# A hybrid attention layer on one core: another attention loop and another spectral loop

## The chip, the cores and the metric

The kernel runs on one core of a Trainium2 chip. The metric is the device time of one execution in microseconds, the median of several runs. In the text PE is TensorE (matmuls), PEld its weight loads, DVE is VectorE, ACT is ScalarE, POOL is GpSimd, and SP is the engine that issues most of the DMAs. SBUF is the on-chip memory of 128 partitions; PSUM holds eight banks of 512 float32 for each partition, into which matmuls write. All data are float32.

## What is computed

The input is four images of 56x56 pixels with 128 channels. One layer adds neighbourhood attention to it, the next adds linear attention and then a convolution with sixteen long filters. Cut to its core:

```python
# x: (4, 56, 56, 128)
q, k, v = heads(gn(x) @ qkv_w.T + qkv_b)              # 4 heads of 32
a = softmax(q . k[7x7 window] * 32**-0.5 + bias)      # 49 weights per pixel
x = x + (a . v[7x7 window]) @ proj_w.T + proj_b

t = tokens(x)                                         # (4, 3136, 128)
n = layernorm(t)
q, k, v = exp(n @ Wq + bq), exp(n @ Wk + bk), n @ Wv + bv
t = t + q @ (k.T @ v)

u = layernorm(t)
for i, frac in enumerate((1, 2, 4, 8)):               # experts, one is chosen
    xi = u[:, : T // frac]
    U_plus, U_minus = fft_convolutions(phi, xi)       # 16 filters each
    s_i = (U_plus * sigma**0.25) @ M_plus[i] + (U_minus * sigma**0.25) @ M_minus[i]
    s_i = s_i + sum(shift(xi, j) @ M_u[i, j] for j in range(3))
t = t + sum_i weight_i * pad(s_i)                     # weights: one-hot
```

## The kernel before

The work has three parts.

**The main part**, image by image (the loop of L928): `project` normalises an image by its groups and makes the queries `qT`, the padded keys `kp` in SBUF and the values, which go to memory as `vpad`. `attend` walks over 35 tiles: 7 rows of tiles with four of 8x12 pixels and one of 8x8. A tile of 96 queries meets 14x18 = 252 keys, in two halves of 126. `mix` adds the projected attention (`add_tokens`, L548 to 557), normalises (`normed`), makes `kv` and `q2` (linear attention), adds that, normalises again, and adds the three taps under the mask `tmask`. `row_transforms` of an image is the first step of its convolution: 7 groups of matmuls L509, each pair of results `xs` going to memory as `xd`. It is a generator; the kv loop of the next image's `mix` takes a step of it every second turn (L896), and the last image's steps run alone.

PSUM in this part is three pools of two buffers: `ps_s` has two pairs of banks, `ps_t` and `ps_m` two single banks each. `bank()` gives project and mix their banks in a turn of three: two from `ps_s`, whose pairs it splits, and one from `ps_m`.

In `attend` a tile goes through these steps: `score` (L738, four matmuls, one per head, into two pairs `sp`); `soften` (L755 adds the bias and takes the negated maximum on DVE; L766 is the exp on ACT, with the sum of a row); `turn_over` (L797, eight transposes into two banks `pt`); `keep_weights` (L808: DVE copies the first half to SBUF, ACT the second); `invert` (L780 reciprocal, L782 a copy on POOL that spreads it, `wide`); `collect` (L819, sixteen matmuls with the values `v_sb`, and L826, which turns `wide` over to the channels), after which DVE copies `rb` (L834) and multiplies into `aT` (L835). The order of PE, DVE, ACT and POOL is written out by hand here (L844): in turn n a tile n+2 is loaded, n-2 is turned over, n is softened in two halves with `keep_weights(n - 2)` between them, n-1 inverted, n-3 collected, and n+1 scored. Everywhere else a scheduler chooses the order of an engine's instructions.

`normed` collects the means and variances of four blocks, then makes their factors at once on DVE with two operations on POOL (L585 and L586, a power), then those of the other three, and normalises all blocks on ACT (L597).

**The spectral loop** (L1070) has 42 iterations, one for each frequency row, and three more to run out. Iteration `it` makes the matrices of the filters, `gt`, for `it`: in each of eight turns `eh`, `matrices` issues 16 matmuls (32 instructions in the profile) into two pairs of banks `pg`, one pair copied by DVE and one by ACT (L1006). `token_points` (L979) transforms the tokens into `us`. `product` (L1016) multiplies `gt` and `us` of iteration `it - 1`: two matmuls for each of 56 points, four instructions in the profile, with 16 columns of `us` as the weights and 128 of `gt` as the moving operand; `j = m2 % 4` chooses the 32 rows of the result. `gather` (L1029) copies 16 rows at a time to `ys`, which goes through memory (`regroup`) to `yg`, and `columns` (L1052) of iteration `it - 3` transforms back to `zs`, which is stored. PE's order is written out by hand.

**The last part** (L1107 on) transforms the rows back and adds the result.

Of the kernel before, what the change touches and what calls it, by code (L numbers as in the profile page):

```python
# [120 lines left out]
def hybrid_kernel(  # L121
# [252 lines left out]
    with main as ph:  # L374
# [5 lines left out]
        ps_s = ph.enter_context(tc.tile_pool(name="ps_s", bufs=2, space=bass.MemoryType.PSUM, reuse_waits="tile"))  # L380
        ps_t = ph.enter_context(tc.tile_pool(name="ps_t", bufs=2, space=bass.MemoryType.PSUM, reuse_waits="tile"))
        ps_m = ph.enter_context(tc.tile_pool(name="ps_m", bufs=2, space=bass.MemoryType.PSUM, reuse_waits="tile"))

        turn, pair = [0], []

        def bank():

            turn[0] = (turn[0] + 1) % 3
            if turn[0] == 2:
                return ps_m.tile([P, 512], F32, tag="m", name="bm")  # L390
            if not pair:
                two = ps_s.tile([P, 2, 512], F32, tag="s", name="bs")
                pair.extend((two[:, 1, :], two[:, 0, :]))
            return pair.pop()
# [98 lines left out]
        def row_transforms(b):  # L493
# [10 lines left out]
            yield  # L504
            for i in range(BR // 4):
# [10 lines left out]
                for s in range(NS):  # L516
                    xs = work.tile([2 * N1, 2, 4, C], F32, name="xs", bufs=2)
                    evacuate(xs.rearrange("p h w c -> p h (w c)"), px[s][: 2 * N1])
                    for wh in range(2):
                        w0 = wh * BR + 4 * i  # L520
                        nc.sync.dma_start(xd[:, w0 : w0 + 4, s, b, :], xs[:, wh])
                yield
# [46 lines left out]
        def normed(acc, add, to):  # L569


            stats = small.tile([P, 2 * NB, 6], F32, name="stats", bufs=2)
            nc.gpsimd.memset(stats[:, 2 * NB - 2 :], 1.0)

            def factors(g0, g1):

                s, n = stats[:, g0:g1], g1 - g0
                v = small.tile([P, 4, 16], F32, name="v")
                total, d, rstd, shift = (v[:, i, :n] for i in range(4))

                nc.vector.tensor_tensor(d, s[:, :, 1], s[:, :, 4], ALU.subtract)
                nc.vector.tensor_tensor(rstd, s[:, :, 2], s[:, :, 5], ALU.add)
                nc.vector.scalar_tensor_tensor(d, d, C / 4.0, d, ALU.mult, ALU.mult)
                nc.vector.tensor_tensor(rstd, rstd, d, ALU.add)
                nc.gpsimd.tensor_scalar(rstd, rstd, 1.0 / C, LN_EPS, ALU.mult, ALU.add)  # L585
                nc.gpsimd.tensor_tensor(rstd, rstd, mhalf[:, :n], ALU.pow)  # L586
                nc.vector.tensor_tensor(total, s[:, :, 1], s[:, :, 4], ALU.add)
                nc.vector.scalar_tensor_tensor(shift, total, -0.5, rstd, ALU.mult, ALU.mult)  # L588
                return rstd, shift

            def normalize(js, g0, rstd, shift):
                r = rows_of(js[0])
                hn = work.tile([P, 2, 2, C], F32, name="hn", bufs=3)
                for g in range(2 * len(js)):
                    jj, f = divmod(g, 2)
                    at = 2 * js[0] - g0 + g
# [4 lines left out]
                        bias=shift[:r, at : at + 1],  # L601
                        scale=rstd[:r, at : at + 1],
# [3 lines left out]
            parts = []  # L606
            for run in (BLOCKS[:4], BLOCKS[4:]):
                for js in run:
                    add(js)
                    r = rows_of(js[0])  # L610
                    for j in js:
                        for f in range(2):
                            nc.vector.bn_stats(
                                stats[:r, 2 * j + f, :], acc[:r, j, f * C : (f + 1) * C]
                            )
                g0, g1 = 2 * run[0][0], 2 * run[-1][-1] + 2
                parts.append((run, g0, *factors(g0, g1)))
            for run, *args in parts:
                for js in run:
                    normalize(js, *args)  # L620
# [91 lines left out]
        def attend(b, qT):  # L712
# [7 lines left out]
            def load(n):  # L720

                ty, x0, qc = tiles[n]
                kc, y0 = qc + KS - 1, ty * QR
                v_sb = work.tile([KMAX, 2, C], F32, name="v_sb", bufs=6)
                for c in range(2):
                    nc.sync.dma_start(
                        v_sb[: KH * kc, c], vpad[b, y0 + c * KH : y0 + (c + 1) * KH, x0 : x0 + kc]
                    )
                state[n] = {"v": v_sb, "nq": QR * qc, "kn": KH * kc}

            def score(n):
                ty, x0, qc = tiles[n]
                t = state[n]
                nq, kn, y0 = t["nq"], t["kn"], ty * QR
                t["sp"] = [ps_s.tile([P, 2, 512], F32, tag="s", name="sp") for _ in range(2)]
                for h in range(NH):
                    hs = slice(h * HD, (h + 1) * HD)
                    nc.tensor.matmul(  # L738
                        t["sp"][h // 2][:nq, h % 2, : 2 * kn],
                        qT[hs, ty, QR * x0 : QR * x0 + nq],  # L740
                        kp[hs, y0 : y0 + KR, x0 : x0 + qc + KS - 1],
# [3 lines left out]
                t["st"] = work.tile([NQ, NH, NK], F32, name="st", bufs=3)  # L745
                t["nmx"] = small.tile([NQ, NH], F32, name="nmx")
                t["sum"] = small.tile([NQ, NH], F32, name="ssum")

            def soften(n, heads):

                t = state[n]
                nq, kn, st = t["nq"], t["kn"], t["st"]
                for h in heads:
# [3 lines left out]
                        t["sp"][h // 2][:nq, h % 2, : 2 * kn],  # L757
                        relb[tiles[n][2]][:, h],
# [4 lines left out]
                        t["nmx"][:nq, h : h + 1],  # L763
                    )
                for h in heads:
# [4 lines left out]
                        bias=t["nmx"][:nq, h : h + 1],  # L770
                        scale=-1.0,
                        accum_out=t["sum"][:nq, h : h + 1],
                    )

            def invert(n):

                t = state[n]
                nq = t["nq"]
                rec = small.tile([NQ, NH], F32, name="rec")
                nc.vector.reciprocal(rec[:nq], t["sum"][:nq])  # L780
                t["wide"] = work.tile([NQ, NH, HD], F32, name="wide", bufs=4)
                nc.gpsimd.tensor_copy(  # L782
                    t["wide"][:nq],
                    rec[:nq].rearrange("q (h o) -> q h o", o=1).to_broadcast([nq, NH, HD]),
                )

            def turn_over(n):

                t = state[n]
                nq, kn, st = t["nq"], t["kn"], t["st"]  # L790
                t["pt"] = []
                for c in range(2):
                    pt = ps_t.tile([P, 512], F32, tag="t", name="pt")[:, : NH * NQ].rearrange(
                        "p (h q) -> p h q", h=NH
                    )
                    for h in range(NH):
                        nc.tensor.transpose(  # L797
                            pt[:kn, h, :nq], st[:nq, h, c * kn : (c + 1) * kn], ident[:nq, :nq]
                        )
                    t["pt"].append(pt)  # L800

            def keep_weights(n):
                t = state[n]
                nq, kn = t["nq"], t["kn"]
                t["p"] = []
                for c, copy in enumerate((nc.vector.tensor_copy, nc.scalar.copy)):
                    pc = work.tile([KMAX, NH, NQ], F32, name=f"p{c}", bufs=2)
                    copy(pc[:kn, :, :nq], t["pt"][c][:kn, :, :nq])  # L808
                    t["p"].append(pc)

            def collect(n):
                ty, x0, qc = tiles[n]
                t = state.pop(n)
                nq, kn = t["nq"], t["kn"]
                po = ps_m.tile([P, 512], F32, tag="m", name="po")
                for c in range(2):
                    for h in range(NH):
                        hs = slice(h * HD, (h + 1) * HD)
                        nc.tensor.matmul(  # L819
                            po[hs, :nq],  # L820
                            t["v"][:kn, c, hs],
                            t["p"][c][:kn, h, :nq],
# [3 lines left out]
                nc.tensor.matmul(  # L826
                    po[:, P : P + nq],
                    t["wide"][:nq].rearrange("q h c -> q (h c)"),
                    ident[:nq, :nq],
                    start=True,  # L830
                    stop=True,
                )
                rb = work.tile([P, NQ], F32, name="rb")
                nc.vector.tensor_copy(rb[:, :nq], po[:, P : P + nq])  # L834
                nc.vector.tensor_tensor(  # L835
                    backwards(aT[:, ty * QR : (ty + 1) * QR, x0 : x0 + qc]),
                    po[:, :nq].rearrange("c (y x) -> c y x", x=qc),
                    rb[:, :nq].rearrange("c (y x) -> c y x", x=qc),
                    ALU.mult,
                )  # L840

            N = len(tiles)
            E = mybir.EngineType
            with tc.manual_schedule(engines={E.PE, E.DVE, E.Activation, E.Pool}):  # L844
                load(0), load(1)
                score(0)
                for n in range(N + 3):
                    if n + 2 < N:
                        load(n + 2)
# [88 lines left out]
        for _ in rows:  # L938
            pass
# [251 lines left out]
```

## Time and profile before

| what | us |
|---|---|
| median of three runs | 2600.92 (2596.2 to 2601.67) |
| the profiled execution: its time | 2596.2 |
| its span, first to last instruction | 2594.2 |
| PE busy, of the span | 2149.8 (83%) |
| DVE busy | 1348.2 (52%) |
| ACT busy | 1077.8 (42%) |
| POOL busy | 144.1 (6%) |
| mean granted clock of TensorE | 0.791 of full |
| attention, image 0: first score to last `aT` | 137 |
| attention, images 1, 2, 3 | 165, 175, 139 |
| spectral loop | 1350 to 2440 |
| last part | 2440 to 2594 |

The page of a profile lists groups of instructions by line, engine and operation. "out<-in" names the tiles; then come the shape, the count, the busy time and the mean time of one in nanoseconds, and last the idle time of the engine just ahead of these instructions with what ended most of it. A slice is one fortieth of the span; a digit is the busy share in tenths.

### The profile page before, as it was taken

The page shows a single profiled execution, that of the slowest core. Times are in us where ns is not written, and L with a number is a line of the kernel's source. Part 1 is how long each engine was busy: PE and PEld are TensorE (multiplying, and loading weights), DVE is VectorE, ACT ScalarE, POOL GpSimd, SP SyncE. Part 2 cuts the span into 40 slices and gives each one's busy share as a digit, 9 for nine tenths or more (in the row PEclk, how much of TensorE's full clock was granted, in tenths as well). Part 3 has the DMA queues.
Part 4 walks back from the last instruction along what each step waited for, and adds up shares of the span by engine and source line. Part 5 has one row for each costly group of instructions (what it writes and reads, how often), then busy time and mean ns, then how long its engine had stood idle before and what let it go on. Part 6 is the DMA issues. An engine that isn't in the chain of part 4 may idle for free.

```text
span 2594.2 us, 66462 instructions
## 1 busy us (share of the span) xinstructions
PE 2149.8 (83%) x28564; PEld 1488.6 (57%) x28564; DVE 1348.2 (52%) x3324; ACT 1077.8 (42%) x2521; POOL 144.1 (6%) x287
## 2 busy tenths in 40 slices
PE   3069977898878987998868888888888888888498
PEld 3036655565645655665536766666676676666222
DVE  5246645464454645664425555556555555655132
ACT  0026542464334633564314555555555555555100
POOL 1110011001110002001000000000000000000000
PEclk8565588557975579656868999999999999999655
DMA  6631004011320113110351333433333343333597
GB/s 167 135 115 33 23 18 118 22 34 30 115 75 22 30 49 102 55 34 12 101 161 38 85 78 79 90 78 84 78 84 79 78 90 78 79 71 64 125 233 196
DMA packets 219512, 210.07 MB, mean 81 GB/s; under 512 B 43154, under 2 KB 187250, under 8 KB 218642
## 3 DMA queue, kind: packets, MB, share of 16 engines
q1 hardware_dynamic: 197850, 189.31, 29.2%
q10 hardware_dynamic: 21368, 16.51, 2.5%
q8 instruction: 224, 3.67, 0.6%
q14 instruction: 70, 0.57, 0.1%
HBM read 116.32 MB, written 89.45 MB: 79 GB/s over the span
## 4 chain that ended last, share of the span: by engine, by line
PE 56%; DVE 19%; ACT 10%; DMA 9%; issue 3%; POOL 1%; ACTq 1%; SPq 0%; DVEq 0%; POOLq 0%
PE pg L997 8%; PE pt L797 7%; PE sp L738 7%; DVE ys L1029 7%; PE py L1016 6%; ACT ys L1029 5%; DVE gt L1006 5%; PE po L819 4%; PE po L826 4%; ACT gt L1006 3%; PE bs L548 3%; PE pz L1052 2%; DMA out_dram<-tl 2%; PE pu L979 2%; PE po L1122 2%
## 5 line engine op out<-in xcount | busy, mean ns | idle before, releaser
L1006 DVE COPY gt<-pg 128x896 f32<-128x896 f32 x336 | 366.7, 1091 | 289.3 <-PE pg L997 278.1
L997 PE MATMUL pg<-v,mats 32*128 32x112 f32 x10752 | 398.0, 285 | 100.8 <-DVE gt L1006 83.9
L997 PEld LDWEIGHTS pg<-v,mats 32*128 32x128 f32 x10752 | 337.7, 190 | 190.1 <-DVE gt L1006 165.0
L1006 ACT COPY gt<-pg 128x896 f32<-128x896 f32 x336 | 304.5, 906 | 244.4 <-PE pg L997 232.4
L1016 PE MATMUL py<-gt,us 128*16 128x128 f32 x9408 | 389.8, 283 | 2.5 <-DVE gt L1006 1.6
L766 ACT ACTIVATE st<-st,nmx 96x252 f32<-96x252 f32 (+1 forms) x560 | 272.6, 488 | 190.5 <-DVE nmx L755 190.5
L1016 PEld LDWEIGHTS py<-gt,us 128*16 128x16 f32 x9408 | 295.0, 112 | 67.4 <-issue 31.1
L1029 DVE COPY ys<-py 16x512 f32<-16x512 f32 (+1 forms) x336 | 209.5, 624 | 160.3 <-ACT ys L1029 156.5
L755 DVE CUSTOM_DVE_ANT_0 st<-sp,relb 96x252 f32<-96x252 f32 (+1 forms) x560 | 203.5, 399 | 73.9 <-PE sp L738 73.5
L1029 ACT COPY ys<-py 16x512 f32<-16x512 f32 (+1 forms) x336 | 174.6, 520 | 149.3 <-DVE ys L1029 141.1
L738 PE MATMUL sp<-kp,qT 32*96 32x252 f32 (+1 forms) x1120 | 195.1, 635 | 30.4 <-DVE nmx L755 29.8
L797 PEld LDWEIGHTS pt<-ident,st 96*126 96x126 f32 (+1 forms) x1120 | 163.8, 216 | 87.4 <-issue 82.4
L797 PE MATMUL pt<-ident,st 96*126 96x96 f32 (+1 forms) x1120 | 201.5, 360 | 0.0
L1122 PE MATMUL po<-z,onto 84*56 84x512 f32 x224 | 125.8, 1066 | 21.1 <-DMA z<-zd 21.1
L1052 PE MATMUL pz<-yg,back 112*112 112x512 f32 x168 | 97.1, 660 | 46.7 <-ACT zs L1059 36.2
L597 ACT ACTIVATE hn<-acc,v 128x128 f32<-128x128 f32 (+1 forms) x208 | 83.0, 482 | 100.7 <-DVE v L588 99.4
L819 PE MATMUL po<-p,v_sb 126*32 126x96 f32 (+1 forms) x2240 | 115.1, 356 | 0.0
L738 PEld LDWEIGHTS sp<-kp,qT 32*96 32x96 f32 (+1 forms) x1120 | 67.3, 237 | 82.3 <-DVE nmx L755 58.4
L808 DVE COPY p<-pt 126x384 f32<-126x384 f32 (+1 forms) x140 | 74.1, 529 | 68.4 <-PE pt L797 64.0
L1131 DVE SCALAR_TENSOR_TENSOR tl<-po,hmask,tl 56x512 f32<-56x512 f32 x56 | 42.0, 750 | 124.3 <-PE po L1122 123.6
L766 ACT ACTIVATION_READ_ACCUMULATOR st<-st,nmx 96x1 f32 (+1 forms) x560 | 105.3, 188 | 0.0
L826 PE MATMUL po<-ident,wide 96*128 96x96 f32 x280 | 101.7, 465 | 0.0
(167 smaller groups left out, 2228.4 us busy)
## 6 DMA issues: line engine op xcount, KB each, us to landing
xd<-xs SPq DMA_DIRECT2D x112, 168.0 KB
xm<-xd SPq DMA_DIRECT2D x84, 224.0 KB
yd<-ys SPq DMA_DIRECT2D x168, 112.0 KB
yg<-yd SPq DMA_DIRECT2D x84, 224.0 KB
zd<-zs SPq DMA_DIRECT2D x84, 224.0 KB
z<-zd SPq DMA_DIRECT2D x14, 1344.0 KB
v_sb<-vpad SPq DMA_DIRECT2D x224, 63.0 KB
vpad<-vt SPq DMA_DIRECT2D x56, 112.0 KB
```

Of the source, the lines that this page charges most:

```text
L738: nc.tensor.matmul(t["sp"][h // 2][:nq, h % 2, : 2 * kn], qT[hs, ty, QR * x0 : QR * x0 + nq], kp[hs, y0 : y0 + KR, x0 : x0 + qc + KS - 1], ...
L755: nc.vector.tensor_tensor_reduce(st[:nq, h, : 2 * kn], t["sp"][h // 2][:nq, h % 2, : 2 * kn], relb[tiles[n][2]][:, h], -1.0, 3.0e38, ALU.a ...
L766: nc.scalar.activation(st[:nq, h, : 2 * kn], st[:nq, h, : 2 * kn], AF.Exp, bias=t["nmx"][:nq, h : h + 1], scale=-1.0, accum_out=t["sum"][: ...
L797: nc.tensor.transpose(pt[:kn, h, :nq], st[:nq, h, c * kn : (c + 1) * kn], ident[:nq, :nq])
L819: nc.tensor.matmul(po[hs, :nq], t["v"][:kn, c, hs], t["p"][c][:kn, h, :nq], start=(c == 0), stop=(c == 1),)
L826: nc.tensor.matmul(po[:, P : P + nq], t["wide"][:nq].rearrange("q h c -> q (h c)"), ident[:nq, :nq], start=True, stop=True,)
L997: nc.tensor.matmul(pg[g // 2][:, g % 2, 2 * N2 * i : 2 * N2 * (i + 1)], mats[rows, 4 * eh + i, :], v[rows], start=True, stop=True,)
L1006: copy(gt[:, :, e0 : e0 + 8, :].rearrange("p m (g i) c -> p g m i c", g=2), pg[q][:, :, : 8 * N2].rearrange("p g (i m c) -> p g m i c", i= ...
L1016: nc.tensor.matmul(py[32 * j : 32 * j + 2 * NSB, slot, :], us[:, 1 - c : 3 - c, :, m2], gt[:, m2, :, c], start=(c == 0), stop=(c == 1),)
L1029: (nc.vector.tensor_copy if j % 2 else nc.scalar.copy)(ys[rows, 4 * q : 4 * q + n], py[rows, :n])
L1052: nc.tensor.matmul(pz, tables_of(m1)[2], yg[:, s * B : (s + 1) * B].rearrange("p k e -> p (k e)"), start=True, stop=True,)
L1122: nc.tensor.matmul(po[64 * q : 64 * q + H].rearrange("p b c -> p (b c)"), onto[:, s], zin[q][:, i, s], start=(s == 0), stop=(s == NS - 1),)
```

## The change

In the main part:

- `ps_s` has three pairs, `ps_t` and `ps_m` one bank each. `bank()` gives one half of three pairs and the bank of `ps_m`, in a turn of four.
- `row_transforms` is no generator; it runs in one go after the next image's `project`, ahead of `attend`.
- `normed` makes the factors for each block, all on POOL, and normalises two blocks behind.
- `attend` writes out only PE's order: first half of `turn_over(n - 2)`, the scores of n, the second half, and `collect(n - 3)`. The weights are divided by their sums on POOL ahead of the transposes, so that `wide`, its matmul and the multiplication with `rb` go. `st` has four buffers, `p0` and `p1` three, `v_sb` five instead of six.

In the spectral loop:

- `pg` has three pairs under one name; of each pair DVE copies one bank and ACT the other, 448 contiguous elements each.
- `gt` is laid out as [128, C, N2, 2] instead of [128, N2, C, 2], so that a copy is contiguous and a product's moving operand steps by 112 elements.
- `us2`, two fixed buffers, has two parts of zeros behind its three, so that the weights have 32 columns and a product writes all its 32 rows. An evacuation is one copy of 128 rows instead of four of 16.
- Eight points follow each `matrices` in turns 0 to 6; both `token_points` and both `columns` stand in turn 7 and share the banks `x` and `y`.

```diff
-        ps_s = ph.enter_context(tc.tile_pool(name="ps_s", bufs=2, space=bass.MemoryType.PSUM, reuse_waits="tile"))
-        ps_t = ph.enter_context(tc.tile_pool(name="ps_t", bufs=2, space=bass.MemoryType.PSUM, reuse_waits="tile"))
-        ps_m = ph.enter_context(tc.tile_pool(name="ps_m", bufs=2, space=bass.MemoryType.PSUM, reuse_waits="tile"))
+        ps_s = ph.enter_context(tc.tile_pool(name="ps_s", bufs=3, space=bass.MemoryType.PSUM, reuse_waits="tile"))
+        ps_t = ph.enter_context(tc.tile_pool(name="ps_t", bufs=1, space=bass.MemoryType.PSUM, reuse_waits="tile"))
+        ps_m = ph.enter_context(tc.tile_pool(name="ps_m", bufs=1, space=bass.MemoryType.PSUM, reuse_waits="tile"))
...
         def bank():
-            turn[0] = (turn[0] + 1) % 3
-            if turn[0] == 2:
+            turn[0] = (turn[0] + 1) % 4
+            if turn[0] == 3:
                 return ps_m.tile([P, 512], F32, tag="m", name="bm")
-            if not pair:
-                two = ps_s.tile([P, 2, 512], F32, tag="s", name="bs")
-                pair.extend((two[:, 1, :], two[:, 0, :]))
-            return pair.pop()
+            return ps_s.tile([P, 2, 512], F32, tag="s", name="bs")[:, 0, :]
...
+            def statistics(js):
+                r, n = rows_of(js[0]), 2 * len(js)
+                stats = small.tile([P, 4, 6], F32, name="stats")
...
+                nc.gpsimd.tensor_tensor(total, s[:, :, 1], s[:, :, 4], ALU.add)
+                nc.gpsimd.tensor_tensor(d, s[:, :, 1], s[:, :, 4], ALU.subtract)
+                nc.gpsimd.tensor_tensor(d, d, d, ALU.mult)
+                nc.gpsimd.tensor_scalar(d, d, C / 4.0, None, ALU.mult)
+                nc.gpsimd.tensor_tensor(rstd, s[:, :, 2], s[:, :, 5], ALU.add)
+                nc.gpsimd.tensor_tensor(rstd, rstd, d, ALU.add)
                 nc.gpsimd.tensor_scalar(rstd, rstd, 1.0 / C, LN_EPS, ALU.mult, ALU.add)
-                nc.gpsimd.tensor_tensor(rstd, rstd, mhalf[:, :n], ALU.pow)
-                nc.vector.tensor_tensor(total, s[:, :, 1], s[:, :, 4], ALU.add)
-                nc.vector.scalar_tensor_tensor(shift, total, -0.5, rstd, ALU.mult, ALU.mult)
+                nc.gpsimd.tensor_tensor(rstd, rstd, mhalf[:r, :n], ALU.pow)
+                nc.gpsimd.tensor_tensor(shift, total, rstd, ALU.mult)
+                nc.gpsimd.tensor_scalar(shift, shift, -0.5, None, ALU.mult)
                 return rstd, shift
...
+            waiting = []
+            for js in BLOCKS:
+                add(js)
+                waiting.append((js, *statistics(js)))
+                if len(waiting) > 2:
+                    normalize(*waiting.pop(0))
...
+                    if h % 2:
+                        nc.vector.reciprocal(rec[:nq, h - 1 : h + 1], ssum[:nq, h - 1 : h + 1])
+                for h in range(NH):
+                    nc.gpsimd.tensor_scalar(
+                        st[:nq, h, : 2 * kn], st[:nq, h, : 2 * kn], rec[:nq, h : h + 1], None, ALU.mult
+                    )
...
+            with tc.manual_schedule(engines={mybir.EngineType.PE}):
+                for n in range(len(tiles) + 3):
+                    if 2 <= n < len(tiles) + 2:
+                        turn_over(n - 2, 0)
+                    if n < len(tiles):
+                        weigh(n)
+                    if 2 <= n < len(tiles) + 2:
+                        turn_over(n - 2, 1)
+                    if n >= 3:
+                        collect(n - 3)
...
             qT = project(acc, b)
-            next(rows, None)
+            if b > 0:
+                row_transforms(b - 1)
...
-            pg = [ps_g.tile([P, 2, 512], F32, tag=f"g{q}", name=f"pg{q}") for q in range(2)]
+            pg = [ps_g.tile([P, 2, 512], F32, tag="g", name="pg") for q in range(2)]
...
-            for q, copy in enumerate((nc.vector.tensor_copy, nc.scalar.copy)):
-                e0 = 16 * eh + 8 * q
-                copy(
-                    gt[:, :, e0 : e0 + 8, :].rearrange("p m (g i) c -> p g m i c", g=2),
-                    pg[q][:, :, : 8 * N2].rearrange("p g (i m c) -> p g m i c", i=4, c=2),
-                )
+            for q in range(2):
+                for g, copy in enumerate((nc.vector.tensor_copy, nc.scalar.copy)):
+                    e0 = 16 * eh + 8 * q + 4 * g
+                    copy(
+                        gt[:, e0 : e0 + 4].rearrange("p i m c -> p (i m c)"), pg[q][:, g, : 8 * N2]
+                    )
...
                 nc.tensor.matmul(
-                    py[32 * j : 32 * j + 2 * NSB, slot, :],
-                    us[:, 1 - c : 3 - c, :, m2],
-                    gt[:, m2, :, c],
+                    py[32 * j : 32 * (j + 1), slot, :],
+                    us.rearrange("p c k m -> p (c k) m")[:, NSB * (1 - c) : NSB * (5 - c), m2],
+                    gt[:, :, m2, c],
                     start=(c == 0),
                     stop=(c == 1),
...
                 for eh in range(8):
                     if it < N1:
                         matrices(it, gts[it], eh)
...
+                    if eh == 7:
+                        for s in range(NS):
+                            if it < N1:
+                                token_points(it, xms[it], us2[it % 2], s)
+                        for s in range(NS):
+                            if 0 <= az < N1:
+                                columns(az, ygs[az], zs, s)
+                    if 0 <= ap < N1 and eh < 7:
+                        if eh % 2 == 0:
+                            py = ps_y.tile([P, 4, C], F32, tag="y", name="py")
+                        for m2 in range(8 * eh, 8 * eh + 8):
+                            product(py, gts[ap], us2[ap % 2], m2)
+                        if eh % 2 or eh == 6:
+                            q, n = eh // 2, 2 if eh == 6 else 4
+                            evacuate(ys[:, 4 * q : 4 * q + n], py[:, :n])
```

## The prediction

> **What bounds the kernel now.** I read the slices of the page first. They show two long stages with different limits: attention with its token work, up to about 1350 us, and the spectral loop, from 1350 to 2440 us.
>
> ```profile
> PE   3069977898878987998868888888888888888498
> PEclk8565588557975579656868999999999999999655
> L1006 DVE COPY gt<-pg 128x896 f32<-128x896 f32 x336 | 366.7, 1091 | 289.3 <-PE pg L997 278.1
> L1029 DVE COPY ys<-py 16x512 f32<-16x512 f32 (+1 forms) x336 | 209.5, 624 | 160.3 <-ACT ys L1029 156.5
> L1029 ACT COPY ys<-py 16x512 f32<-16x512 f32 (+1 forms) x336 | 174.6, 520 | 149.3 <-DVE ys L1029 141.1
> L826 PE MATMUL po<-ident,wide 96*128 96x96 f32 x280 | 101.7, 465 | 0.0
> ```
>
> The first line is busy TensorE, the second its granted clock. The spectral loop has the full clock and is still not at nine tenths; DVE and ACT take turns there over the `ys` copies. Next, what the first matmul of each L997 group waits for, which is the PE's only large loss in that loop:
>
> ```profile
> its engine sat idle before it (us, times) until:
>   DVE gt L1006: 248.9, 381
> ```
>
> The PE loses 248.9 us in 42 iterations, 5.9 us each, because both bank pairs of `pg` must be copied out (1091 ns on DVE, 906 on ACT) before the next group may write. The starts of successive L1052 matmuls stand 25.18 us apart, so the loop is 42 x 25.18 us plus its edges.
>
> Then the attention windows, whose columns are the stretch, the length, the busy times of the five engines, the clock, the DMA share and GB/s:
>
> ```profile
> 200.00:250.00 50.00, 50.00 (x447) 33.29 (x448) 32.44 (x156) 31.53 (x119) 3.75 (x13) 0.50 0.11 33
> 750.00:800.00 50.00, 40.87 (x265) 23.60 (x264) 21.20 (x103) 22.09 (x80) 2.60 (x9) 0.50 0.07 21
> 1700.00:1750.00 50.00, 44.03 (x998) 34.38 (x993) 29.72 (x36) 25.38 (x41) 0.00 (x0) 1.00 0.37 82
> ```
>
> In image 0 (first line) the PE is busy throughout at half clock: this stage is PE bound, 3.78 us a tile. In the second line only four score halves at a time find a slot, and a tile takes 5.6 us. Measured from first score to last write of `aT`, the four images take 137, 165, 175 and 139 us, 616 in all. The timeline of one tile gives the latencies that I use below:
>
> ```profile
> 222.86 1.17 PE L738 MATMUL sp<-kp,qT 32*96 32x252 f32 x8
> 223.96 1.54 PE L797 MATMUL pt<-ident,st 96*126 96x96 f32 x8
> 224.06 0.42 DVE L755 CUSTOM_DVE_ANT_0 st<-sp,relb 96x252 f32<-96x252 f32 x1 [0.55 <-PE sp L738]
> 224.58 0.51 ACT L766 ACTIVATE st<-st,nmx 96x252 f32<-96x252 f32 x1 [1.26 <-DVE nmx L755]
> 225.09 0.49 ACT L766 ACTIVATE st<-st,nmx 96x252 f32<-96x252 f32 x1
> 225.59 0.48 ACT L808 COPY p<-pt 126x384 f32<-126x384 f32 x1
> ```
>
> [...]0.50 in every attention window, with the PE 50.00 or 40.87 of 50 us busy. I therefore price the new attention loop at half clock too. [...]Before, the moving operand of a product steps by 8 bytes[...]; after, by 448 bytes[...]. The nearest is the weight load of L1016, 16 columns at 224 bytes: 112 ns mean, 106 to 108 mostly, against 93 that the contiguous loads extrapolate to (187 ns for 128 columns, 173 for 112). That fits a doubled price for each column, or a fixed smallest load; it decides nothing. [...]the trace gives 722 ns for a POOL add of 128x256 and 682 for DVE's of 128x512[...].
>
> **The change part by part.**
>
> *Spectral loop (gain).* One eh is now L997's 32 instructions, 1.09 us of issue, and 32 product instructions where there were 28 in 1.10 us: 1.215 us. Without any wait that is 2.305 us. The 16 copies of 128x896 become 32 of 128x448: about 0.62 us on DVE (the same shape takes 619 ns at L987) and 0.54 on ACT (between 359 ns for 256 columns and 573 for 512). The two halves of a pair are built with ACT's copy waiting for DVE's, as ACT's L988 now waits for L987. There are three pair buffers and two are used in each eh, so the second pair of eh+1 has to wait for the first pair of eh: 1.19 (first matmul to first copy, from the trace) + 0.62 + 0.05 + 0.54 + 0.06 = 2.46 us, slightly over 2.305. Seven of them are 17.2 us. The eighth eh has no products; it has a group (1.09), both token transforms (1.07 each), and both columns, which share their banks and so wait for the `us` copies on DVE and the sign changes on ACT: 5.35 us. The sum is 22.5 us against 25.18 (22 to 23.5 as the copies pack). Over 41 steady iterations that is -109, with the last iterations -113 us. The evacuations fall from 16 copies of 16 rows to 4 of 128 rows; DVE then has 12.9 us and ACT 11.1 in an iteration, neither a bound.
>
> *Attention (loss).* Removed are the 280 matmuls of L826 (0.67 us in a tile with its load), POOL's 289 ns copy, and one of DVE's two 257 ns operations. Added are four POOL multiplications of 96x252 per tile. Nearest row 722 ns for two inputs of 256, 615 for a copy: 0.45 to 0.75 each, 1.8 to 3.0 in a tile; hidden beside a cycle of 5 us, a bound only above 1.25 each. PE work falls to about 3.5 us a tile. But `pt` now has one bank instead of two, and the order on ACT is no longer written out: as built, the copy of the second half of tile n-2 stands behind all four exps of tile n, in all 140 tiles. The first turn of tile n-1 needs that bank. So the cycle is: four transposes with the switch of shape 0.84 (half of 1.54, plus 0.07) + scores to the first reduction 1.20 (222.86 to 224.06) + to the first exp 0.52 + four exps at 0.50, 2.0 + the copy 0.48 + signals 0.13 = 5.17 us. What is queued behind this copy on ACT is the next tile's exps, which wait for nothing else of it. Every fifth tile is smaller (64x196, exp 451 ns), about 4.5; mean 5.04. An image is 35 x 5.04 + 2 to fill = 178 us, the four 714 against 616: +98, say +100. The range is +60 (signals and exps overlapping better) to +130 (POOL or the `v_sb` loads, now in the same tile, adding to the chain).
>
> *Row transforms.* Taken out of the kv phase, they run in one turn after the next image's project, with all their evacuations ahead of attention's first reductions in DVE's and ACT's queues, and their transfers on SP's queue ahead of the first `v_sb` loads. Alone they are bound by transfers: the last one shows a pair of `xs` every 4.1 us. Seven pairs are 28.7 us, some 25 exposed, three times: 75. Where they are now they stretch the kv phase by 19.8 + 19.2 + 27.8 = 67 us. Net +8 (-10 to +20).
>
> *Statistics.* In the first norm of a mix, factors come from DVE and two POOL powers (2904 and 1957 ns). Now every block has ten POOL operations, about 3.55 us (nine at 0.2 to 0.3 each, and a power of 128x4 at about 1.03, drawn from 1957 ns at 10 and 2904 at 16). Seven blocks make 25 us before the last factors, where the kv phase starts 22 us after the last `aT` now; +5 per image, +20. The second norm is held by the PE's three taps (3.1 us a block), which hide this chain, and loses a stall of 5 us for factors: -6 in all.
>
> *Banks.* In project and mix four banks turn where there were six: +5 (0 to +10), since most groups there are evacuated by then.
>
> The sum on the profiled execution's 2596.2 us: -113 + 100 + 8 + 20 - 6 + 5 = +14, 2610. The median shown is 2600.9, 4.7 above that execution, so 2615 us.
>
> **The rivals.**
>
> A. *The strided operand is slow.* For it: [...]the 112 ns load. Against: an instruction's 128 columns take 270 to 283 ns here, so the read may have room. If the products take twice as long in their moving part, 32 instructions are 2.07 us, the eh 3.16, the iteration 7 x 3.16 + 5.35 = 27.5: +95 on the loop instead of -113, 2823 us; at half this penalty 2720.
>
> B. *Attention's new chain is shorter (the other side: faster).* The place is ACT's copy of the second half before the next first turn. It decides the sign from 4.9 us a tile downwards (5.04 less the 14 us spread over 140 tiles). At a clock of 1.0, which takes 0.37 from the turn and 0.5 from the scores, or with the copy ahead of two of the exps, the cycle is about 4.3 us: 4 x 152 = 608, -8 instead of +100; total 2507. For it: less PE work, less waiting for slots (three pairs, none given to `bank()` halves). Against: a clock of 0.50 in every window.
>
> C. *POOL is the bound*, above 1.25 us a multiplication: at 1.5, 6 us a tile, 35 x 4 x 1 more, 2750 us. Against: 722 ns for a heavier operation.
>
> **How the numbers follow.** The likeliest case, two large parts that nearly cancel: 0.48, 2615 us, its own range 2560 to 2665 from the bounds above. A: 0.27. B: 0.22. C: 0.03. 0.2%, about 5 us, is what a measurement of this kernel tells from no change. Faster: 0.15 of the likeliest case and nearly all of B, 0.28. Within: 0.05. Slower: 0.67. The range goes from 2535 to 2770: it leaves out the stronger half of A and the lower half of B.
>
> **What would show it.** Spectral: starts of the column matmuls 22 to 23.5 us apart, and a product instruction with the cadence of now; if A holds, the PE is busy all through at 27 us. Attention: ACT's exps directly ahead of its `p1` copy, the first turn waiting for that copy, 5.0 us a tile; if B, a PE with no waits or tiles under 4.5. Kv starting 26 us or more after the last `aT`. A granted clock above 0.5 in attention would make the prediction wrong, as would products slower than 1.3 us for eight points.

## The result and the profile after

The changed kernel takes 2822.18 us (median of four runs, 2815.72 to 2827.99) against 2601.24: a ratio of 1.0854, 95% interval 1.0826 to 1.0881. It is 221 us slower, where 14 were forecast; the time is that of rival A, 2823 us. Its profiled execution has a span of 2819.1 us, 224.9 above the one before. In the later comparisons a few executions of the kernel before (two of 23 in the first), and one of four of each of two kernels with its attention, were some 50 us shorter than the rest, so kernels are compared below by their medians, which lie among the rest.

Read off both traces in the same way, the difference goes to the following parts (us):

| part | before | after | difference | forecast |
|---|---|---|---|---|
| attention, four images | 616.3 | 716.2 | +99.9 | +100 |
| from each image's last `aT` to the next attention or the loop | 553.6 | 593.6 | +40.0 | +27 |
| spectral loop, first L997 (now L942) to the end of the last column matmul | 1089.9 | 1173.2 | +83.3 | -113 |
| ahead of attention, and the last part | 334.4 | 336.1 | +1.7 | 0 |

So one term, the loop's, is wrong by nearly 200 us. The page of the changed kernel shows busy PE and granted clock by slices, then groups with their count, busy time, mean in ns and idle time ahead.

```profile
PE   3066778666876668766777999999999999999698
PEclk7565578555875559655877999999999999999855
L961 PE MATMUL py<-gt,us 128*32 128x128 f32 x9408 | 617.9, 409 | 3.3 <-ACT ys L183 1.4
L952 DVE COPY gt<-pg 128x448 f32<-128x448 f32 x672 | 388.3, 619 | 479.4 <-PE pg L942 475.1
L758 POOL TENSOR_SCALAR st<-st,rec 96x252 f32<-96x252 f32 (+1 forms) x560 | 486.0, 883 | 368.7 <-DVE rec L756 215.0
L952 ACT COPY gt<-pg 128x448 f32<-128x448 f32 x672 | 357.9, 535 | 618.1 <-DVE gt L952 618.1
L942 PE MATMUL pg<-v,mats 32*128 32x112 f32 x10752 | 398.5, 285 | 14.8 <-ACT gt L952 8.3
L770 PE MATMUL pt<-ident,st 96*126 96x96 f32 (+1 forms) x1120 | 233.2, 359 | 214.6 <-ACT p L774 162.6
```

The product instructions before:

```profile
L1016 PE MATMUL py<-gt,us 128*16 128x128 f32 x9408 | 389.8, 283 | 2.5 <-DVE gt L1006 1.6
```

The spectral loop now shows nines: PE no longer waits for the copies, as the three pairs were to bring about. It takes longer all the same, because a product instruction has a mean of 409 ns where it had 283. The `gt` copies cost what was forecast (619 and 535 ns; 620 and 540). In attention the slices show the reverse: sixes where eights and nines stood, with the transposes (L770) waiting. Two windows say the same, the first in attention, the second in the loop, with the columns that the prediction explains:

```profile
200.00:250.00 50.00, 34.03 (x324) 20.34 (x320) 24.01 (x121) 23.53 (x91) 34.70 (x40) 0.50 0.09 26
1700.00:1750.00 50.00, 49.45 (x908) 36.28 (x904) 23.18 (x40) 20.36 (x39) 0.00 (x0) 1.00 0.37 82
```

In the loop the PE is busy 49.45 of 50 us, 44.03 before, and does less: 908 matmul instructions against 998. Successive column groups start 27.2 us apart (median), against 25.18.

The timeline of one turn `eh` of that loop, from its products to the next group of L942:

```profile
1708.20 2.10 PE L961 MATMUL py<-gt,us 128*32 128x128 f32 x32
1708.37 1.16 DVE L952 COPY gt<-pg 128x448 f32<-128x448 f32 x2 [0.46 <-PE pg L942]
1709.03 1.07 ACT L952 COPY gt<-pg 128x448 f32<-128x448 f32 x2 [2.12 <-DVE gt L952]
1710.23 0.98 PEld L942 LDWEIGHTS pg<-v,mats 32*128 32x128 f32 x32 [0.41 <-issue]
```

From the start of the 32 product instructions to the next group are 2.03 us. The copies of both pairs end at 1710.10, ahead of that group, so nothing is waited for here. The forecast had 1.215 us for these 32.

And one tile of attention:

```profile
230.86 3.58 POOL L758 TENSOR_SCALAR st<-st,rec 96x252 f32<-96x252 f32 x4 [2.40 <-DVE aT L792]
235.80 0.49 ACT L747 ACTIVATE st<-st,nmx 96x252 f32<-96x252 f32 x1
236.19 0.19 ACT L747 ACTIVATION_READ_ACCUMULATOR st<-st,nmx 96x1 f32 x1
236.28 0.35 ACT L774 COPY p<-pt 98x256 f32<-98x256 f32 x1
236.41 0.16 DVE L756 RECIPROCAL rec<-ssum 96x2 f32<-96x2 f32 x1 [0.66 <-ACT st L747]
236.75 0.61 PEld L770 LDWEIGHTS pt<-ident,st 96*126 96x126 f32 x4 [2.00 <-POOL st L758]
236.78 0.87 PE L770 MATMUL pt<-ident,st 96*126 96x96 f32 x4 [1.68 <-POOL st L758]
241.92 0.87 PE L770 MATMUL pt<-ident,st 96*126 96x96 f32 x4 [1.75 <-ACT p L774]
```

The fourth exp comes first, then ACT's copy of the second half, to 236.63, then at 236.75 the next first turn. The releaser is given as POOL, but that tile's multiplications ran from 230.86 to 234.44 and had been over for 2.3 us. It is the copy that came last, and the first turn of the tile after, at 241.92, is put down to it.

### The profile page after: what moved, and what is told of

It reads as the page before. It is cut to its first block, busy times and chain, and to the rows that moved or that the text cites. A ratio compares the mean times of both kernels' runs of the same rounds, so it can differ in the third digit from the quotient of the medians.

```text
span 2819.1 us, 67241 instructions
## 1 busy us (share of the span) xinstructions
PE 2265.4 (80%) x28284; PEld 1525.4 (54%) x28284; DVE 1220.4 (43%) x3354; ACT 992.9 (35%) x2563; POOL 697.8 (25%) x1229
## 3 DMA queue, kind: packets, MB, share of 16 engines
q1 hardware_dynamic: 197850, 189.31, 27.2%
## 4 chain that ended last, share of the span: by engine, by line
PE 62%; ACT 12%; DMA 9%; DVE 8%; POOL 4%; issue 4%; SPq 1%; ACTq 1%; DVEq 0%; POOLq 0%
PE py L961 21%; PE pg L942 13%; ACT st L747 8%; PE sp L723 5%; PE pt L770 4%; PE bs L543 3%; PE pz L987 3%; DMA xd<-xs 3%; PE po L1066 2%; DVE st L736 2%; ACT gt L952 2%; PE bs L824 2%; DMA z<-zd 1%; ACT p L774 1%; POOL st L758 1%
## 5 line engine op out<-in xcount | busy, mean ns | idle before, releaser
L961 PE MATMUL py<-gt,us 128*32 128x128 f32 x9408 | 617.9, 409 | 3.3 <-ACT ys L183 1.4
L952 DVE COPY gt<-pg 128x448 f32<-128x448 f32 x672 | 388.3, 619 | 479.4 <-PE pg L942 475.1
L758 POOL TENSOR_SCALAR st<-st,rec 96x252 f32<-96x252 f32 (+1 forms) x560 | 486.0, 883 | 368.7 <-DVE rec L756 215.0
L952 ACT COPY gt<-pg 128x448 f32<-128x448 f32 x672 | 357.9, 535 | 618.1 <-DVE gt L952 618.1
L961 PEld LDWEIGHTS py<-gt,us 128*32 128x32 f32 x9408 | 403.7, 145 | 107.6 <-ACT ys L183 2.4
L942 PEld LDWEIGHTS pg<-v,mats 32*128 32x128 f32 x10752 | 338.2, 190 | 169.1 <-issue 89.4
L942 PE MATMUL pg<-v,mats 32*128 32x112 f32 x10752 | 398.5, 285 | 14.8 <-ACT gt L952 8.3
L770 PE MATMUL pt<-ident,st 96*126 96x96 f32 (+1 forms) x1120 | 233.2, 359 | 214.6 <-ACT p L774 162.6
L770 PEld LDWEIGHTS pt<-ident,st 96*126 96x126 f32 (+1 forms) x1120 | 159.0, 206 | 346.8 <-POOL st L758 252.1
L723 PE MATMUL sp<-kp,qT 32*96 32x252 f32 (+1 forms) x1120 | 162.3, 648 | 3.7 <-DVE xs L185 2.3
L505 PE MATMUL px<-uin,into 28*84 28x512 f32 x224 | 76.7, 960 | 36.3 <-DVE xs L185 20.9
L1066 PEld LDWEIGHTS po<-z,onto 84*56 84x56 f32 x224 | 32.9, 206 | 114.6 <-issue 98.0
L543 PE MATMUL bs<-mu,ut 128*128 128x128 f32 (+1 forms) x528 | 80.6, 319 | 12.4 <-DVE ut L185 6.2
L756 DVE RECIPROCAL rec<-ssum 96x2 f32<-96x2 f32 x280 | 44.7, 160 | 103.6 <-ACT st L747 89.9
```

Source lines behind the costliest of these rows:

```text
L543: nc.tensor.matmul(pt[:r, o : o + C], lhs[:, t0 : t0 + 2 * r - 1 : 2], rhs, start=(i == 0), stop=(i == len(terms) - 1),)
L723: nc.tensor.matmul(sp[h // 2][:nq, h % 2, : 2 * kn], qT[hs, ty, QR * x0 : QR * x0 + nq], kp[hs, y0 : y0 + KR, x0 : x0 + kc], start=True, s ...
L758: nc.gpsimd.tensor_scalar(st[:nq, h, : 2 * kn], st[:nq, h, : 2 * kn], rec[:nq, h : h + 1], None, ALU.mult)
L770: nc.tensor.transpose(pt[:kn, h, :nq], st[:nq, h, c * kn : (c + 1) * kn], ident[:nq, :nq])
L942: nc.tensor.matmul(pg[g // 2][:, g % 2, 2 * N2 * i : 2 * N2 * (i + 1)], mats[rows, 4 * eh + i, :], v[rows], start=True, stop=True,)
L952: copy(gt[:, e0 : e0 + 4].rearrange("p i m c -> p (i m c)"), pg[q][:, g, : 8 * N2])
```

## The experiments

### The step of the moving operand, or the width of the weights

Both changed in L961: the step from 8 to 448 bytes, the weights from 16 to 32 columns. Three kernels change one at a time. The first keeps everything of the changed kernel but the step, the layout of `gt` included; its products therefore meet other elements of `gt` than the computation asks for, as in every kernel here that changes the step alone.

```diff
-                    gt[:, :, m2, c],
+                    gt.rearrange("p e m c -> p (e m c)")[:, 256 * m2 + c : 256 * m2 + c + 255 : 2],
```

> The changed kernel, with only the step of a product's moving operand set from 448 to 8 bytes (the layout of gt and all copies stay, so the products meet other elements of gt than the reference's). If the step makes a product slow (theory: 32 product instructions 2.06 us at 448 bytes, 1.22 at 8), the loop falls from 27.5 to about 22.5 us an iteration and the kernel to about 2615 us. If the 32 columns of weights are the cause (rival), nothing changes: 2822 us.

Measured: 2608.82 us (20 runs, 2600.25 to 2613.28), 213 less than the changed kernel. The loop's median iteration fell from 27.2 to 21.95 us. A block of 32 products goes to the next group in 1.19 us. The instructions have a median of 281 ns here and of 404 in the changed kernel:

```profile
L961 PE MATMUL py<-gt,us x9408: 273/281/357, 1523.8 to 2434.3; 128*32 128x128 f32 x196
```

```profile
L961 PE MATMUL py<-gt,us x9408: 393/404/462, 1521.7 to 2648.8; 128*32 128x128 f32 x196
```

The timeline at the short step, two eh:

```profile
1701.27 1.32 PE L942 MATMUL pg<-v,mats 32*128 32x112 f32 x32
1702.51 1.25 PE L961 MATMUL py<-gt,us 128*32 128x128 f32 x32
1703.69 1.16 PE L942 MATMUL pg<-v,mats 32*128 32x112 f32 x32
1704.78 1.24 PE L961 MATMUL py<-gt,us 128*32 128x128 f32 x32
```

Now the third-pair wait of the prediction is there, and it is small. The first group takes 1.24 us to its products, the second 1.09: in the first the matmuls into the second pair start 0.15 us late, at 1701.43, just after ACT's copy out of that pair, which ended at 1701.38. Two eh last 4.7 us, 2.35 each, where 2.46 was forecast.

The other way round, in the kernel before:

```diff
-                    gt[:, m2, :, c],
+                    gt.rearrange("p m e c -> p (m e c)")[:, 2 * m2 + c : 2 * m2 + c + 14225 : 112],
```

> The kernel before, with only the step of a product's moving operand set from 8 to 448 bytes (the products meet other elements of gt). If the step is slow: 28 product instructions 1.85 us instead of 1.10; with 1.09 of L997 that is 2.94 an eh against 2.63 now, so some 2.5 us an iteration more and about 2700 us in all. If the weights' width is the cause: no change, 2601 us.

Measured: 2803.15 us, ratio to the kernel before 1.0764 (1.0744 to 1.0784). The direction is the step's; the size is twice what was expected. The expectation took 2.63 us as a fixed eh, as though each hid 0.44 us of waiting. In the trace of before seven of the eight blocks of 28 products take, with the wait behind them, 1.10 to 1.35 us, and one takes 2.66, so most eh had little waiting in which a longer block could hide. With the long step the seven take 1.9 to 2.05 us and the one 2.82, and the iteration grows from 25.18 to 29.95 us.

Then the width alone:

```diff
-                    us[:, 1 - c : 3 - c, :, m2],
+                    us.rearrange("p c k m -> p (c k) m")[:, NSB * (1 - c) : NSB * (5 - c), m2],
```

> The kernel before, with only the weights of a product widened from 16 to 32 columns (16 of zeros, and 32 rows written). If the step is the cause of the slow products: no change, 2601 us to within 10, the weight loads going from 106 to about 134 ns behind the matmuls. If the width is: products about 400 ns instead of 283 and about 2700 us.

Measured: 2613.01 us, 9 above the kernel before (2603.72 in that comparison), the iteration 25.4 instead of 25.18 us. The two kinds of product by tile, with the smallest, the median and the largest duration in ns, as above; first the kernel before with the step, then with the width:

```profile
L1016 PE MATMUL py<-gt,us x9408: 383/396/441, 1389.2 to 2628.0; 128*16 128x128 f32 x196
```

```profile
L1020 PE MATMUL py<-gt,us x9408: 273/280/436, 1386.4 to 2435.5; 128*32 128x128 f32 x196
```

396 ns with 16 columns and the long step, 280 with 32 columns and the short one. The weight loads grew from 112 to 143 ns in the second, beside the matmuls, and the kernel by only 9 us. The step is the cause, shown in both kernels.

### How long a step

Three more steps in the changed kernel, one execution each: 12, 16 and 444 bytes (3, 4 and 111 in place of the 2 that ends the slice in the first experiment, with the slice's other numbers to fit).

> The changed kernel with the products' moving operand at a step of 12 bytes (other elements of gt than the reference's). [...]between 8 and 16 bytes[...]: a product block of 1.6 to 2.0 us, an iteration of 25 to 27.3 us, 2730 to 2815 us. If the price starts only at a long step: 1.19 us a block and about 2609 us.

> The changed kernel with the products' moving operand at a step of 16 bytes (other elements of gt). [...]2.03 us a block as at 448 bytes, 27.2 us an iteration, about 2822 us. If the price starts only at a long step (rival): 1.19 us and about 2609 us.

> The changed kernel with the products' moving operand at a step of 444 bytes (other elements of gt). [...]the same as at 448 bytes, 2.03 us a block, about 2822 us. If 448 = 7 x 64 is slow[...] (rival): faster, down to 1.2 us and 2609 us.

Measured: 2707.03, 2827.62 and 2814.23 us. The product instructions, in the order 12, 16, 444:

```profile
L961 PE MATMUL py<-gt,us x9408: 338/348/429, 1524.2 to 2535.0; 128*32 128x128 f32 x196
```

```profile
L961 PE MATMUL py<-gt,us x9408: 405/414/458, 1521.6 to 2654.7; 128*32 128x128 f32 x196
```

```profile
L961 PE MATMUL py<-gt,us x9408: 398/407/448, 1520.1 to 2640.8; 128*32 128x128 f32 x196
```

With 281 ns at 8 bytes and 404 at 448, a step of 16 bytes already costs all of it (414), and 444 bytes no more (407), so 448 is no special case. At 12 bytes it is half: 67 ns above 281, against 133 at 16; the kernel stayed below the 2730 to 2815 us expected there. Whether the price grows evenly between 8 and 16 bytes or in jumps, these points do not tell, and what it comes from, no run here shows.

### What sets a tile of attention

The copy of the second half is moved ahead of the exps, by writing ACT's order out; PE's order stays (`E` is `mybir.EngineType`).

```diff
-            with tc.manual_schedule(engines={mybir.EngineType.PE}):
+            with tc.manual_schedule(engines={E.PE, E.Activation}):
...
                         turn_over(n - 2, 1)
+                    if n < len(tiles):
+                        soften(n)
                     if n >= 3:
                         collect(n - 3)
```

> The changed kernel with ACT's order in attention written out: the copy of the second transposed half of tile n-2 ahead of the four exps of tile n; PE's order stays. If that copy behind the exps sets the 5.1 us of a tile (theory), the tile falls to about 4.0 us, then held by POOL's four multiplications (3.58 us in the profile) and PE (3.5): the four images 716 to about 570 us, the kernel about 2680 us (2660 to 2720). If POOL's multiplications hold the tile already (rival, as the profile's releasers have it for half of the first turns): no change, 2822 us.

Measured: 2793.46 us; attention 683.3 us instead of 716.2, where about 570 was expected. The copy did set the tile, but only 0.24 us of it was to be had: a second limit stood right behind. In its trace:

```profile
232.04 3.58 POOL L764 TENSOR_SCALAR st<-st,rec 96x252 f32<-96x252 f32 x4 [1.09 <-DVE rec L762]
234.78 0.42 PE L775 MATMUL pt<-ident,st 96*126 96x96 f32 x1 [0.44 <-POOL st L764]
235.67 0.42 PE L775 MATMUL pt<-ident,st 96*126 96x96 f32 x1 [0.47 <-POOL st L764]
236.02 0.41 PEld L723 LDWEIGHTS sp<-kp,qT 32*96 32x96 f32 x8 [0.17 <-issue]
236.13 0.56 DVE L779 COPY p<-pt 126x384 f32<-126x384 f32 x1 [1.87 <-PE pt L775]
236.60 0.15 DVE L762 RECIPROCAL rec<-ssum 96x2 f32<-96x2 f32 x1
236.92 3.58 POOL L764 TENSOR_SCALAR st<-st,rec 96x252 f32<-96x252 f32 x4 [1.30 <-DVE rec L762]
```

The transposes of the first half now wait one by one for POOL's multiplications; the DVE copy of that half follows, and behind it in DVE's queue stands the reciprocal for the next tile's multiplications. From 232.04 to 236.92, after 4.88 us, POOL starts again.

So the reciprocal is put ahead of that copy, with DVE's order written out too. It is also made once for the four heads of a tile instead of twice for two, so POOL now starts after the fourth exp; the two changes were not tried apart.

```diff
+            with tc.manual_schedule(engines={E.PE, E.Activation, E.DVE}):
                 for n in range(len(tiles) + 3):
+                    if 1 <= n <= len(tiles):
+                        divide(n - 1)
```

> As e6_copy_first, and DVE's order written out too, with one reciprocal per tile at the head of the next turn, ahead of the copy of a first half. Theory: in e6_copy_first a second loop took over at 4.88 us a tile: POOL's four multiplications (3.58 us), then the first half's turn, its copy on DVE, the second reciprocal behind that copy, and POOL again. With the reciprocal ahead of the copy POOL works nearly without a break: 3.6 to 4.0 us a tile, the four images 683 to some 510 to 570 us, the kernel 2620 to 2680 us. If another limit near 4.9 us stays (rival): 2793 us.

Measured: 2765.84 us, attention 658.3. Again in the right direction and short of the expected 510 to 570. POOL's timeline:

```profile
238.02 3.59 POOL L767 TENSOR_SCALAR st<-st,rec 96x252 f32<-96x252 f32 x4 [1.63 <-PE sp L723]
242.18 3.59 POOL L767 TENSOR_SCALAR st<-st,rec 96x252 f32<-96x252 f32 x4 [0.57 <-PE pt L778]
246.49 3.02 POOL L767 TENSOR_SCALAR st<-st,rec 64x196 f32<-64x196 f32 x4 [0.73 <-DVE rec L765]
251.07 7.26 POOL L767 TENSOR_SCALAR st<-st,rec 96x252 f32<-96x252 f32 x8 [1.56 <-PE sp L723]
259.96 3.59 POOL L767 TENSOR_SCALAR st<-st,rec 96x252 f32<-96x252 f32 x4 [1.63 <-PE sp L723]
```

Five tiles take 21.94 us, 4.39 each, 3.5 of them POOL's own work. It still pauses. On PE the scores of tile n+2 stand behind the first turn of tile n, which waits for POOL, and the exps that follow those scores are what POOL waits for next. That this loop over two tiles is the rest was read from the trace and not tried.

### The two repairs together, and the best of both kernels

> As e7_divide_first, with gt in the layout of before and its products at a step of 8 bytes. The sum of the two repairs: e7_divide_first less the 213 us that the step was worth, 2410 to 2470 us; equal to or below e4_combined (2470) if the attention loop with the division on POOL can match the order written out by hand of before (616 us for four images).

Measured: 2548.42 us: the two repairs add up within 4 us (2765.84 less 213 is 2553), but attention at 657.8 us stays 41 above the order of before. The expected 2410 to 2470 took it that the reordered attention alone would come to 2620 to 2680.

The other combination is the main part of before with the changed loop, `gt` kept in the old layout. Against the changed loop its copies read:

```diff
-                        gt[:, e0 : e0 + 4].rearrange("p i m c -> p (i m c)"), pg[q][:, g, : 8 * N2]
+                        gt[:, :, e0 : e0 + 4, :],
+                        pg[q][:, g, : 8 * N2].rearrange("p (i m c) -> p m i c", i=4, c=2),
```

> The main part of the kernel before with the changed spectral loop, whose gt keeps the layout of before ([128, N2, C, 2]): copies of 448 elements into runs of eight, products at a step of 8 bytes. Theory (attention is the other half of the loss, and only the step spoils the loop): 22.5 us an iteration, 2601 - 113 = about 2490 us. If copies of 128x448 into runs of eight are slower than contiguous ones, or the waits for the third pair weigh more: 23.5 to 25, 2530 to 2595.

Measured: 2469.58 us, 134 below the kernel before (2603.72), the fastest of all, with 21.96 us an iteration. That is 20 below the expected 2490, since the loop gains 132 us and not 113. The copies, in the window 1700 to 1900 us:

```profile
L1015 DVE COPY gt<-pg 128x448 f32<-128x448 f32 x146 | 84.4, 620 | 67.6 <-PE pg L1005 67.6
L1015 ACT COPY gt<-pg 128x448 f32<-128x448 f32 x145 | 77.1, 533 | 92.2 <-DVE gt L1015 92.2
```

620 and 533 ns into runs of eight elements, 619 and 535 into one run: the contiguous destination bought nothing, and the products paid for it. Here the products meet the right elements of `gt`, and the iteration is that of the first experiment (21.95).

### The 40 us between the attentions

The row transforms put back into the kv loop:

> The changed kernel with the row transforms back in steps within the next image's kv loop. Between the attentions the changed kernel loses 40 us to the one before. If the row transforms in one turn are most of that (about 30 us exposed three times, against 67 us in the kv loop): 20 to 30 us less, about 2795 us. If they cost as much in either place (rival, with the rest going to the statistics and the four banks): within 10 of 2822 us.

Measured: 2825.03 us (2814.75 to 2827.2), 3 above the changed kernel. To within a few us they cost as much in either place.

The factors of a norm in two batches again:

> The changed kernel with the factors of a norm made in two batches per norm as before (DVE and two POOL powers), in place of ten POOL operations a block. The statistics were priced at +20 us in the first norms and -6 in the second; if that is right the kernel falls by about 14 us, to some 2808 us. If the 33 us that are left between the attentions without the row transforms are all the statistics': by 30, to about 2790. If they belong to the four banks in turn: no change, 2822.

Measured: 2789.81 us, 32 below. The statistics are the larger part of the 40. What the rest is, some 8 us, was not taken apart; 5 were forecast for the banks. In the changed kernel the idle time ahead of ACT's normalising, from the view of the tile `hn` (us, times), and then in this one:

```profile
  POOL v L586: 140.3, 54
```

```profile
  DVE v L583: 79.6, 8
```

One wait per block (54 for 56 blocks) in place of one per norm (8 for 8), and 61 us more of it; about half comes through to the end.

## Why the prediction was wrong

**The products, the step that failed.** "32 product instructions where there were 28 in 1.10 us: 1.215 us" carried the old pace over to a step of 448 bytes instead of 8, and so put the change of the step at nothing. (The count alone gives 1.26; the slip is small.) It measured 2.03, and 1.19 at the old step. An eh is then 1.09 + 2.03 = 3.12 us, against 2.35 at the old step; over seven of them that is 5.4 us, about the 5.2 that lie between iterations of 27.2 and 21.95.

The prediction had this case as rival A, with 2.07 us a block, 27.5 us an iteration and 2823 us in all, and gave it 0.27. A's cause, the step, is right; that its total is met to 1 us is luck, since its loop was 12 us too dear (+95 against +83) and the part between the attentions 13 too cheap. The evidence for A was in the trace: the weight load of 16 columns at 224 bytes took 106 to 108 ns, where the two contiguous loads that the prediction names (187 ns for 128 columns, 173 for 112) extrapolate to 89, an estimate (its 93 is a slip). The alternative that it left open, a fixed smallest load, falls with the 32 columns of the third experiment: 31 ns for 16 more columns (112 to 143 ns), against 14 between the contiguous loads. So a column took 1.9 ns at that step against 0.9, about double. The argument against, that an instruction of 270 to 283 ns leaves room for its reads, looked at the wrong duration: the instructions overlap, and 28 of them in 1.10 us is one in every 39 ns.

**The PE's loss in the loop of before: misread.** The 248.9 us that the prediction calls the PE's loss to the copies is the idle time of two engines added up, matmuls 83.9 and weight loads 165.0:

```profile
L997 PE MATMUL pg<-v,mats 32*128 32x112 f32 x10752 | 398.0, 285 | 100.8 <-DVE gt L1006 83.9
L997 PEld LDWEIGHTS pg<-v,mats 32*128 32x128 f32 x10752 | 337.7, 190 | 190.1 <-DVE gt L1006 165.0
```

By the starts of the blocks about 2.5 us an iteration were lost there, not 5.9. The forecast did not rest on it, as it was built up from the blocks.

**The rest of the loop: right, slightly dear.** This holds for the copies of 0.62 and 0.54 us (619 and 535 ns), the serial copies of a pair, the wait for the third pair, 5.35 us for the last eh (5.34 in the changed kernel's trace, from 1701.77 to 1707.11), and 22.5 us an iteration without the step (21.95). At the old step the loop is 133 us shorter than before, where 113 were forecast.

**Attention: right in size and in its mechanism, wrong about what stands behind it.** 714 us were forecast, 716.2 came, and taking the copy from behind the exps did shorten the tile. But POOL was called hidden below 1.25 us a multiplication, which counts its own work alone. A multiplication was put at 0.45 to 0.75 us and measured 912 ns (96x252), and with the turn, the copy and the reciprocal around it POOL's loop lay 0.24 us below the bound. Rival B had the copy ahead of two of the exps at 608 us; the reordered kernel has it ahead of all four, and reached 683.

**Between the attentions: +27 forecast, +40.** The row transforms are right within the run's noise (+8; about 0 here). The statistics, +20 and -6, are about +30, half of it in each norm. From the last `aT` to the end of `q2`, the first norm's stretch, the four images take 206 us with the chain on POOL and 191 with batches: +15. From there to the next attention or the loop, the second norm's stretch, they take 387 and 372: +15 again. So the -6 was the wrong term: "The second norm is held by the PE's three taps (3.1 us a block), which hide this chain" did not hold.

**The clock: right.** It was 0.50 in the attention window above and 1.00 in that of the loop. What holds it at half in attention, no run here shows.

## What to carry to other kernels

Ahead of giving a copy a contiguous destination, count what reads the tile: here the copies ran at the same speed into runs of eight elements (620 and 533 ns, against 619 and 535 into one run), while a float32 moving operand stepping by 448 bytes instead of 8 made a block of products 1.7 times as long (2.03 against 1.19 us). When a duration is carried over from an old row to a new instruction, each property that changes (shape, step, width) needs a row of its own; a weak sign in the trace, such as a weight load that is 17 to 19 ns too long, can be followed up before it is called undecided. And when one link of a loop is taken out, look up what stands next: here three limits lay at 4.98, 4.73 and 4.39 us a tile (24.88, 23.64 and 21.94 us for five, by POOL's starts).

## What was not expected

- The surplus of a product's float32 moving operand over a step of 8 bytes was half there at 12 bytes, all there at 16, and no larger at 444 and 448: 281, 348 and 414 ns at 8, 12 and 16 bytes, 407 at 444, 404 at 448.
- In the changed kernel POOL multiplies 96x252 by one number per partition in 912 ns, while it adds two tiles of 128x256 in 728: the operation with one tensor less is the slower one here.
- Weights of 32 columns in place of 16 lengthen their load from 112 to 143 ns and the kernel by 9 us only.
